# Planner durations of the attention heads, keys of image 1's attention and input projections, and delta's projections paired in two row halves of TensorE

## The chip, the cores and the metric

The kernel runs on one core of a Trainium2 chip. Its metric is device time in microseconds (us), the median of several runs. A core has these engines: TensorE (PE, matrix products and transposes through a 128 x 128 array, results in PSUM), VectorE (DVE), ScalarE (ACT), GpSimd (POOL), and SyncE (SP), which here issues every transfer between memory and the core. Each engine works through its own list of instructions in order and waits at an instruction until the semaphores it needs are there.

## The reference, cut to what matters

Two images of 48 x 48 tokens with 768 channels. Layer 0 is neighbourhood attention, layer 1 a selective scan in both directions. Everything is float32.

```python
def attention(x):                      # 12 heads of 64, keys: the 7 x 7 neighbourhood
    q, k, v = split(x @ w_qkv)
    attn = softmax(q * 64 ** -0.5 . k[neighbours])
    return (attn . v[neighbours]) @ w_out

def scan_branch(x, z):                 # forward; once more on the reversed tokens
    x = silu(depthwise_conv4(x))       # 1536 channels, 2304 tokens
    dt, B, C = split(x_proj_w @ x)     # 48, 16, 16 rows
    delta = softplus(dt_proj_w @ dt + dt_proj_b)
    h[t] = exp(delta[t] * A) * h[t-1] + delta[t] * x[t] * B[t]   # 16 states per channel
    return (sum_n(h * C) + x * Dp) * silu(z)

x = x + attention(group_norm(x))
x = x + out_proj(scan_branch(in_proj(group_norm(x))) + reversed_scan_branch(...))
```

## The kernel before

**Tiling.** The scan works in units. A unit is one tile of 128 channels (`k`, 12 tiles) in one chunk of 384 tokens (`i`, 6 chunks), in one direction (`back`), of one image (`b`): 2 x 2 x 6 x 12 = 288 units, in this order. Image 0 forward is units 0 to 71, image 0 backward 72 to 143, image 1 forward 144 to 215, image 1 backward 216 to 287. A unit has four groups of four states. For each group (`scan`, `group`) the buffer `hb` is filled with delta * x * B (line 1254, on DVE or on POOL), ACT makes exp(delta * A) for each state into the PSUM buffers `da` (line 1276), DVE scans two states at a time (line 1287), POOL multiplies by C (line 1302), and PE adds the states up by transposing them into the bank `py` (line 1319). ACT takes `py` out to `yt` (line 1345). In the backward direction PE turns the sum of both directions back (line 1372), and DVE multiplies by silu(z) (line 1382).

**Delta.** For every three tiles (`KB`) `deltas_of` fetches `u` and the 49 rows (48 and a bias) of the weights `dtw`, multiplies them on PE with the rows `dt` of the chunk (line 1180), one product of 49 x 128 by 49 x 384 for each tile, and ACT copies each result out (line 1186). Softplus over the three (line 1191) needs another table of ACT functions, so there are two table loads about it. The results of line 1180 use the PSUM pool `mm`, which has two banks. The same two banks serve all projections, and, in image 1's attention, its scores, transposes and weighted values too (`BESIDE`).

**Attention.** `project` makes q, k and v of a tile of 384 tokens, `core` and `block` fetch what a block of 8 x 16 queries needs, and `heads` computes two columns of queries of two heads: scores on PE (line 784, two heads in the two row and column halves of the array), a masked maximum on DVE (line 794), exponentials with their sum on ACT (line 800), the reciprocal on DVE (line 815), the scaling on ACT or DVE (lines 843, 849), transposes on PE (line 825), their copy (line 831), the weighted values on PE (line 879), and their copy (line 893). Image 0's attention comes before the scan and has the scan's buffers (`FIRST`). Image 1's attention runs beside image 0's scan. After it come image 1's input projections with the convolution (`in_proj`: PE line 387, ACT line 957, DVE line 964, ACT line 990) and their projections to dt, B and C (`x_proj`).

**What sets the order.** Each operation is recorded with `add(engine, ns, fn, key, reads, writes, ...)`: an assumed duration, a key in units (when it is due), and what it reads and writes. `Order.run` then plans all engines together. It takes the operation that can start first by the assumed durations, ranks by start and key, looks 2.5 units ahead of the oldest unfinished unit, and allots buffers. In the program the instructions of each engine stand in the planned order; on the chip they start when their waits allow it. A fill of groups 1 to 3 may go to DVE or POOL, as the plan finds one free first (`alt`). Where PE would be idle for more than 800 ns in the plan, filler transposes are put there (line 1520). Assumed durations come from `mm`, `act` and `dve`, plus a constant written at the place.

The keys around the change, with lines of the file before:

```python
    A0, A1, P1 = (-56, -16), (50, 118), 118          # attention of image 0, of image 1, input projections
    ...
            attention(b, *A1, True, BESIDE)
    ...
            start = P1 + 12 * i if b else 9 * (i - 1) - 4
            end = start + (ND - 2 if b else 8)
```

Of the kernel before, what the change touches and what calls it, by code (L numbers as in the profile page):

```python
# [16 lines left out]
P = 128  # L17
# [13 lines left out]
NKEY = WR * WC  # L31
# [3 lines left out]
UU = 2  # L35
# [6 lines left out]
RK = 48  # L42
XD = RK + 2 * NS
CL = 384
CHUNKS = [(l, CL) for l in range(0, L, CL)]
# [205 lines left out]
def tile_kernel(  # L251
# [282 lines left out]
    def attention(b, start, end, job, T):  # L534
# [234 lines left out]
        def heads(n, p, i, u, kcs, ks, qs, vs, vat, mask, to, key):  # L769
# [20 lines left out]
            for v in range(UU):  # L790

                def masked(v=v):

                    nc.vector.tensor_tensor_reduce(  # L794
                        pr[:, v, :], scv(v), mask[:, v * NKEY : (v + 1) * NKEY], -1.0, 3.0e38,
                        ALU.add, ALU.min, sm[:, v : v + 1],
                    )
# [7 lines left out]
                add("DVE", dve(NKEY) + 160, masked, key, r=[sc, mask], w=[(pr, v), (sm, v)], **S)  # L805
                add(
                    "ACT", act(NKEY, 1) + 230, exponentials, key, r=[(pr, v), (sm, v)],
                    w=[(pr, v), (sm, UU + v)], **S,
                )
# [44 lines left out]
            if job:  # L854
                add("PE", UU * NK * 110 + 60, lambda: turned(range(UU)), key, r=[pr], w=[pt, pT], **S)
                add(
                    "ACT", act(UU * NK * P) + 30, lambda: taken(range(UU), nc.scalar.copy), key, r=[pt],
                    w=[pT], **S,
# [14 lines left out]
            def weighted():  # L873
# [11 lines left out]
            marks["pv"] = add(  # L885
                "PE", 900, weighted, key, r=[*((x[0], x[1]) for x in vs), pT], w=[po, to], **S
            )
# [11 lines left out]

            add("ACT" if job else "DVE", act(P) + 60, kept, key, r=[po], w=[to], **S)  # L900

# [7 lines left out]
    def in_proj(b, i, start, end, conv=True, gate=True, nk=KB, tags=("uz",), banks=("mm",), proj=None):  # L909
# [78 lines left out]
        def finish(k0, nk, uz, dsts, key):  # L988
# [3 lines left out]

            add("ACT", 2600 + act(len(dsts) * nk * cl), silu, key, r=[uz], w=[uz], job=True)
            for s, dst in enumerate(dsts):
# [162 lines left out]
    def deltas_of(ch, k0, x):  # L1157
# [17 lines left out]
        )  # L1175
        for j in range(KB):
            acc = ps("mm", f"dl_{n}_{j}")
            add(
                "PE", mm(1, cl),
                lambda j=j, acc=acc: nc.tensor.matmul(  # L1180
                    acc[:, c], w[:, j * P : (j + 1) * P], dt[:, c], start=True, stop=True
                ),
                at + 0.01 * j, r=[dt, w, u], w=[acc, (dl, j)], early=EARLY,
            )
            add(
                "ACT", act(cl), lambda j=j, acc=acc: nc.scalar.copy(dl[:, j, c], acc[:, c]),  # L1186
                at + 0.01 * j, [acc], [(dl, j)], early=EARLY,
            )

# [202 lines left out]
    def chunk(b, back, i, at):  # L1392

        l0, cl = CHUNKS[i]
        s = f"{b}_{back}_{i}"
        dt = sb("dt", [RK + 1, CL], s)
        src = xd[back][b]
        add(
            "SP", 400, lambda: nc.sync.dma_start(dt[:, :cl], src[: RK + 1, l0 : l0 + cl]), at - 1.4,
            [(src, cols(l0, cl))], [dt], size=RK * cl * 4,  # L1400
        )
        bc = []
# [54 lines left out]
    for b in range(nb):  # L1457
# [113 lines left out]
```

## Time and profile before

| | |
|---|---|
| Time, median of 3 runs | 7049.78 us (7040.85 to 7054.37) |
| Profiled execution | 7040.0 us |
| Its span, from first to last instruction | 7038.2 us |
| Mean granted clock of TensorE | 0.976 |
| Instructions | 108877 |
| Scans on DVE (line 1287) | 2304, mean 1749 ns |
| Fills (line 1254) | 650 on DVE, mean 1746 ns; 502 on POOL, mean 3203 ns |
| Multiplies on POOL (line 1302) | 1152, mean 3186 ns |
| Delta's projections (line 1180) | 576 records (two for each product) |
| Filler transposes (line 1520) | 5124 |

A row of the profile's groups names line, engine, operation, what is written from what, the shapes and the count, then the busy time and the mean of one, then the idle time of the engine just before and what ended it. The mean of one includes a tail that overlaps with the next instruction of the same engine; from start to start two scans are 1.66 us apart. PE means products, PEld the loading of their stationary operand. Idle time costs only where it is on the path that sets the end.

### The profile page before, as it was taken

The numbers are of one execution on the slowest core, as the hardware profiler recorded it, in microseconds if no ns is written. First come the engines' busy times: TensorE is split into PE (matmuls) and PEld (weight loads), VectorE is DVE, ScalarE is ACT, GpSimd is POOL, SyncE is SP. The second block draws the span as 40 slices with busy tenths as digits, with TensorE's granted clock in tenths as the row PEclk, the third lists the DMA queues.
The fourth block names the chain that finished last, engine by engine and source line by source line (L and its number), as shares of the span: only waits on it lengthen the run. The fifth ranks groups of instructions, "written<-read, shape, count | busy, mean of one in ns | idle before, by whom it ended". The sixth has DMA issues, their size and how long they took to land. (4 is left out here: it accounts for less than half of the span.)

```text
span 7038.2 us, 108877 instructions
## 1 busy us (share of the span) xinstructions
PE 6280.1 (89%) x40140; PEld 4878.2 (69%) x40140; DVE 5990.5 (85%) x6102; ACT 4851.3 (69%) x10516; POOL 5468.5 (78%) x1958
## 2 busy tenths in 40 slices
PE   8999899899899989899988888888888898999888
PEld 5666656666667767666766666666678887777777
DVE  1343459999999989878899999999999999999998
ACT  1222248878887777677877777788876667777774
POOL 0000019898889989777889999999999999999997
PEclk9999999999999999999999999999999999999999
DMA  6666454544565455555542443343466676655553
GB/s 194 185 214 190 143 174 131 153 137 133 162 190 162 148 165 166 161 175 155 179 152 87 137 138 89 95 143 114 139 179 191 175 218 198 192 176 160 163 171 104
DMA packets 1348293, 1115.48 MB, mean 158 GB/s; under 512 B 137840, under 2 KB 1338000, under 8 KB 1347728
## 3 DMA queue, kind: packets, MB, share of 16 engines
q1 hardware_dynamic: 1347760, 1108.50, 52.6%
q8 instruction: 318, 5.21, 0.3%
q14 instruction: 215, 1.76, 0.1%
HBM read 895.34 MB, written 213.57 MB: 158 GB/s over the span
## 5 line engine op out<-in xcount | busy, mean ns | idle before, releaser
L1287 DVE TENSOR_TENSOR_SCAN hb<-da,hb 128x772 f32<-128x772 f32 x2304 | 3923.6, 1749 | 200.1 <-ACT da L1276 148.8
L1302 POOL TENSOR_TENSOR hb<-hb,bc 128x1536 f32<-128x1536 f32 x1152 | 3652.7, 3186 | 379.4 <-DVE hb L1287 287.9
L1276 ACT ACTIVATE da<-dlt,A 128x384 f32<-128x384 f32 x4608 | 2677.4, 584 | 962.5 <-DVE hb L1287 884.9
L1319 PE MATMUL py<-ident,hb 128*128 128x128 f32 x13824 | 1750.0, 279 | 313.5 <-POOL hb L1302 306.6
L1319 PEld LDWEIGHTS py<-ident,hb 128*128 128x128 f32 x13824 | 1566.1, 143 | 570.5 <-POOL hb L1302 471.7
L1254 POOL TENSOR_TENSOR hb<-u,bc 128x1544 f32<-128x1544 f32 x502 | 1606.8, 3203 | 48.7 <-PE py L1319 42.6
L1254 DVE TENSOR_TENSOR hb<-du,bc 128x1544 f32<-128x1544 f32 x650 | 1131.3, 1746 | 37.3 <-ACT du L1231 27.5
L1204 POOL TENSOR_TENSOR u<-dlt,u 128x384 f32<-128x384 f32 x288 | 263.6, 917 | 478.0 <-ACT dlt L1191 386.9
L1520 PE MATMUL py<-ident 128*128 128x128 f32 x5124 | 630.8, 277 | 0.0
L387 PE MATMUL mm_xin<-xc,w_x 128*128 128x390 f32 x1656 | 592.6, 501 | 29.8 <-DVE uz_u L964 12.6
L387 PE MATMUL mm_z<-xc,w_z 128*128 128x384 f32 x1728 | 607.6, 492 | 6.3 <-ACT dlt L1186 3.8
L1520 PEld LDWEIGHTS py<-ident 128*128 128x128 f32 x5124 | 586.8, 143 | 17.3 <-issue 13.6
L387 PE MATMUL mm_out<-stage_y,w_o 128*128 128x192 f32 x3168 | 558.0, 330 | 18.9 <-DMA w_o<-in_w_opT 6.5
L387 PEld LDWEIGHTS mm_out<-stage_y,w_o 128*128 128x128 f32 x3168 | 519.0, 193 | 30.5 <-ACT dlt L1186 10.6
L930 POOL MEMSET xc<- 128x18 f32 x4 | 0.5, 118 | 630.0 <-PE mm_v L387 630.0
L964 DVE SCALAR_TENSOR_TENSOR uz_u<-mm_xin,conv_w,uz_u 128x384 f32<-128x384 f32 x792 | 427.9, 610 | 45.6 <-ACT uz_u L957 44.0
L387 PEld LDWEIGHTS mm_xin<-xc,w_x 128*128 128x128 f32 x1656 | 306.3, 193 | 230.2 <-issue 28.8
L387 PE MATMUL mm_qk<-xc_xn,w_qk 128*128 128x384 f32 x1296 | 452.8, 495 | 8.7 <-DVE sm L794 2.6
L387 PEld LDWEIGHTS mm_z<-xc,w_z 128*128 128x128 f32 x1728 | 314.8, 192 | 192.4 <-issue 9.4
L387 PEld LDWEIGHTS mm_qk<-xc_xn,w_qk 128*128 128x128 f32 x1296 | 238.6, 192 | 161.8 <-issue 15.9
L1260 ACT COPY bc<-state 128x8 f32<-128x8 f32 x960 | 183.0, 196 | 143.9 <-DVE hb L1254 68.3
L800 ACT ACTIVATE pr<-pr,sm 128x196 f32<-128x196 f32 x432 | 194.0, 450 | 126.4 <-DVE sm L794 124.8
(163 smaller groups left out, 6454.8 us busy)
## 6 DMA issues: line engine op xcount, KB each, us to landing
w_o<-in_w_opT SPq DMA_DIRECT2D x264, 384.0 KB
bc<-xdf SPq DMA_DIRECT2D x96, 768.0 KB
bc<-xdb SPq DMA_DIRECT2D x96, 768.0 KB
w_qk<-in_w_qkv SPq DMA_DIRECT2D x144, 384.0 KB
w_x<-in_w_inT SPq DMA_DIRECT2D x144, 384.0 KB
w_z<-in_w_inT SPq DMA_DIRECT2D x144, 384.0 KB
w_ao<-in_w_out SPq DMA_DIRECT2D x72, 384.0 KB
u<-uf SPq DMA_DIRECT2D x48, 576.0 KB
```

What stands on the lines that cost most here:

```text
L387: nc.tensor.matmul(acc[:m, o0 : o0 + cl], wb[:, wi, wo : wo + m], xb[:, xi, xo : xo + cl], start=c == 0, stop=c == n - 1,)
L800: nc.scalar.activation(pr[:, v, :], pr[:, v, :], AF.Exp, bias=sm[:, v : v + 1], scale=-1.0, accum_out=sm[:, UU + v : UU + v + 1],)
L930: nc.gpsimd.memset(xc[:, :, : a - lo], 0.0)
L964: nc.vector.scalar_tensor_tensor(u, px[:, at[j] : at[j] + cl], q["conv_w"][:, k, j : j + 1], u, ALU.mult, ALU.add,)
L1204: lambda j=j: nc.gpsimd.tensor_mul(u[:, j, h], dl[:, j, c], u[:, j, h]), at + 0.06 + 0.25 * j,
L1254: on.tensor_mul(cells(hb, SG), by.unsqueeze(1).to_broadcast([P, SG, W]), bc[g].ap)
L1260: "ACT", 98, lambda: nc.scalar.copy(bc[g][:, :, ends], was), now - 0.4,
L1276: lambda: nc.scalar.activation(cells(da, 2)[:, j % 2, h], dl[:, jd, c], AF.Exp, scale=q["A"][:, k, i : i + 1]),
L1287: lambda: nc.vector.tensor_tensor_scan(flip(hb[at2]), flip(da[:, : 2 * W]), flip(hb[at2]), 0.0, ALU.mult, ALU.add),
L1302: lambda: nc.gpsimd.tensor_mul(cells(hb, SG)[:, :, h], cells(hb, SG)[:, :, h], bc[NSG + g][:, :, c]),
L1319: nc.tensor.matmul(py[:tp, t * P : (t + 1) * P], cells(hb, SG)[:, j, h][:, tb[t]], ident, start=False, stop=g == NSG - 1 and j == SG - 1 a ...
L1520: nc.tensor.matmul(marks["py"][:, CL : CL + P], ident, ident, start=False, stop=False, is_transpose=True, skip_group_check=True,)
```

## The change

The change has three parts. None alters what is computed.

1. The assumed durations in `heads` are other constants, and so are those of the silu in `in_proj` and of the product u * delta on POOL. They alter the plan, not the instructions themselves.
2. Image 1's attention is keyed from unit 46 to 124 (78 units) where it was 50 to 118 (68), and image 1's input projections begin at 124 with 11 units between chunks where they began at 118 with 12.
3. The weights `dtw` and the rows `dt` are fetched twice, to partitions 0 to 48 and to partitions 64 to 112. Of a group of three tiles the first two are multiplied in one operation of the plan, tile 0 from the lower half of the rows and tile 1 from the upper half, into two banks of `mm`; the third is alone, in the lower half. Before, each of the three was an operation of its own.

```diff
+ROW = 64
...
-                add("DVE", dve(NKEY) + 160, masked, key, ...)
+                add("DVE", dve(NKEY) + 22, masked, key, ...)
-                    "ACT", act(NKEY, 1) + 230, exponentials, key, ...
+                    "ACT", act(NKEY, 1) + 130, exponentials, key, ...
-                        "DVE", 198,
+                        "DVE", 70 if job else 150,
-                        "ACT", act(NKEY, 1) + 40,
+                        "ACT", act(NKEY, 1) + 35,
-                    "ACT", act(UU * NK * P) + 30, lambda: taken(range(UU), nc.scalar.copy), ...
+                    "ACT", act(UU * NK * P), lambda: taken(range(UU), nc.scalar.copy), ...
-                "PE", 900, weighted, key, ...
+                "PE", 640 if job else 750, weighted, key, ...
-            add("ACT" if job else "DVE", act(P) + 60, kept, key, ...)
+            add("ACT" if job else "DVE", act(P) if job else 230, kept, key, ...)
...
-            add("ACT", 2600 + act(len(dsts) * nk * cl), silu, key, ...)
+            add("ACT", 2750 + act(len(dsts) * nk * cl), silu, key, ...)
...
-        u, w = sb("u", [P, KB, CL + 2], n, KB), sb("dtw", [RK + 1, KB * P], n)
+        u, w = sb("u", [P, KB, CL + 2], n, KB), sb("dtw", [ROW + RK + 1, KB * P], n)
...
-            nc.sync.dma_start(w.ap, q["dtT"][:, k0 * P : (k0 + KB) * P])
+            for r in (0, ROW):
+                nc.sync.dma_start(w[r : r + RK + 1], q["dtT"][:, k0 * P : (k0 + KB) * P])
...
-        for j in range(KB):
-            acc = ps("mm", f"dl_{n}_{j}")
-            add(
-                "PE", mm(1, cl),
-                lambda j=j, acc=acc: nc.tensor.matmul(
-                    acc[:, c], w[:, j * P : (j + 1) * P], dt[:, c], start=True, stop=True
-                ),
-                at + 0.01 * j, r=[dt, w, u], w=[acc, (dl, j)], early=EARLY,
-            )
-            add("ACT", act(cl), lambda j=j, acc=acc: nc.scalar.copy(dl[:, j, c], acc[:, c]), ...)
+        for j0 in range(0, KB, 2):
+            js = range(j0, min(j0 + 2, KB))
+            accs = [ps("mm", f"dl_{n}_{j}") for j in js]
+
+            def raw(js=js, accs=accs):
+                for j, acc in zip(js, accs):
+                    r = slice(j % 2 * ROW, j % 2 * ROW + RK + 1)
+                    nc.tensor.matmul(
+                        acc[:, c], w[r, j * P : (j + 1) * P], dt[r, c], start=True, stop=True
+                    )
+
+            add(
+                "PE", mm(1, cl) * (1.6 if len(js) > 1 else 1.2), raw, at + 0.01 * j0, r=[dt, w, u],
+                w=[*accs, *((dl, j) for j in js)], early=EARLY,
+            )
+            for j, acc in zip(js, accs):
+                add("ACT", act(cl), lambda j=j, acc=acc: nc.scalar.copy(dl[:, j, c], acc[:, c]), ...)
...
-                "POOL", 960,
+                "POOL", 850,
                 lambda j=j: nc.gpsimd.tensor_mul(u[:, j, h], dl[:, j, c], u[:, j, h]), ...
...
-        dt = sb("dt", [RK + 1, CL], s)
+        dt = sb("dt", [ROW + RK + 1, CL], s)
-        add("SP", 400, lambda: nc.sync.dma_start(dt[:, :cl], src[: RK + 1, l0 : l0 + cl]), at - 1.4, ...)
+        def rows():
+            for r in (0, ROW):
+                nc.sync.dma_start(dt[r : r + RK + 1, :cl], src[: RK + 1, l0 : l0 + cl])
+
+        add("SP", 800, rows, at - 1.4, ...)
...
-    A0, A1, P1 = (-56, -16), (50, 118), 118
+    A0, A1, P1 = (-56, -16), (46, 124), 124
...
-            start = P1 + 12 * i if b else 9 * (i - 1) - 4
+            start = P1 + 11 * i if b else 9 * (i - 1) - 4
```

More of the change, by code (lines that the diff above doesn't have):

```diff
@@ L803, in exponentials @@
                     )
-                add("DVE", dve(NKEY) + 160, masked, key, r=[sc, mask], w=[(pr, v), (sm, v)], **S)
+                add("DVE", dve(NKEY) + 22, masked, key, r=[sc, mask], w=[(pr, v), (sm, v)], **S)
                 add(
-                    "ACT", act(NKEY, 1) + 230, exponentials, key, r=[(pr, v), (sm, v)],
+                    "ACT", act(NKEY, 1) + 130, exponentials, key, r=[(pr, v), (sm, v)],
                     w=[(pr, v), (sm, UU + v)], **S,
@@ L856, in heads @@
                 add(
-                    "ACT", act(UU * NK * P) + 30, lambda: taken(range(UU), nc.scalar.copy), key, r=[pt],
+                    "ACT", act(UU * NK * P), lambda: taken(range(UU), nc.scalar.copy), key, r=[pt],
                     w=[pT], **S,
@@ L885, in heads @@
             marks["pv"] = add(
-                "PE", 900, weighted, key, r=[*((x[0], x[1]) for x in vs), pT], w=[po, to], **S
+                "PE", 640 if job else 750, weighted, key, r=[*((x[0], x[1]) for x in vs), pT], w=[po, to], **S
             )
@@ L898, in kept @@
                 )
-            add("ACT" if job else "DVE", act(P) + 60, kept, key, r=[po], w=[to], **S)
+            add("ACT" if job else "DVE", act(P) if job else 230, kept, key, r=[po], w=[to], **S)
         project(0)
@@ L991, in silu @@
                 nc.scalar.preload_act_table_set("natural_log_exp_and_others")
-            add("ACT", 2600 + act(len(dsts) * nk * cl), silu, key, r=[uz], w=[uz], job=True)
+            add("ACT", 2750 + act(len(dsts) * nk * cl), silu, key, r=[uz], w=[uz], job=True)
             for s, dst in enumerate(dsts):
@@ L1175, in deltas_of @@
         )
-        for j in range(KB):
-            acc = ps("mm", f"dl_{n}_{j}")
-            add(
-                "PE", mm(1, cl),
-                lambda j=j, acc=acc: nc.tensor.matmul(
-                    acc[:, c], w[:, j * P : (j + 1) * P], dt[:, c], start=True, stop=True
-                ),
-                at + 0.01 * j, r=[dt, w, u], w=[acc, (dl, j)], early=EARLY,
-            )
-            add(
-                "ACT", act(cl), lambda j=j, acc=acc: nc.scalar.copy(dl[:, j, c], acc[:, c]),
-                at + 0.01 * j, [acc], [(dl, j)], early=EARLY,
-            )
+        for j0 in range(0, KB, 2):
[7 more added lines that the diff above has]
+                    )
+            add(
+                "PE", mm(1, cl) * (1.6 if len(js) > 1 else 1.2), raw, at + 0.01 * j0, r=[dt, w, u],
+                w=[*accs, *((dl, j) for j in js)], early=EARLY,
+            )
+            for j, acc in zip(js, accs):
+                add(
+                    "ACT", act(cl), lambda j=j, acc=acc: nc.scalar.copy(dl[:, j, c], acc[:, c]),
+                    at + 0.01 * j, [acc], [(dl, j)], early=EARLY,
+                )
         def softplus():
@@ L1395, in chunk @@
         s = f"{b}_{back}_{i}"
-        dt = sb("dt", [RK + 1, CL], s)
+        dt = sb("dt", [ROW + RK + 1, CL], s)
         src = xd[back][b]
[L1398 to L1401, printed above, removed]
+        def rows():
+            for r in (0, ROW):
+                nc.sync.dma_start(dt[r : r + RK + 1, :cl], src[: RK + 1, l0 : l0 + cl])
+        add("SP", 800, rows, at - 1.4, [(src, cols(l0, cl))], [dt], size=2 * RK * cl * 4)
         bc = []
```

## The prediction

> **What bounds the kernel now.** I read the page's parts 1 and 2 first. The first fence has the busy sums, then PE's and DVE's busy tenths in 40 slices of 176 us.
>
> ```profile
> PE 6280.1 (89%) x40140; PEld 4878.2 (69%) x40140; DVE 5990.5 (85%) x6102; ACT 4851.3 (69%) x10516; POOL 5468.5 (78%) x1958
> PE   8999899899899989899988888888888898999888
> DVE  1343459999999989878899999999999999999998
> ```
>
> PE's busy time includes 5124 filler transposes (line 1520), so it is no measure of need. DVE is lightly used in the first six slices (image 0's attention, PE's own stretch), is at 9 almost everywhere afterwards, and dips in slices 14 to 19. I mapped time to units of scan work (a unit is one tile of 128 channels in one chunk, 288 in all) by putting the scans of the trace beside the scans in DVE's instruction order: unit 84 starts at 2814.0 us, unit 108 at 3405.4. A unit takes 18.9 us in the last stages and 24.6 us between those two points. The next view is the stretch view for units 84 to 107, and for comparison units 144 to 155 (columns: length, then busy time of PE, PE loads, DVE, ACT, POOL, then clock and DMA).
>
> ```profile
> core 0: us, PE busy (x) PEld busy (x) DVE busy (x) ACT busy (x) POOL busy (x), PEclk, DMA share, GB/s
> 2814.00:3405.00 591.00, 542.03 (x3815) 405.29 (x3813) 480.73 (x543) 431.93 (x1102) 457.04 (x163) 0.97 0.53 163
> 4201.40:4450.30 248.90, 211.76 (x1435) 170.65 (x1434) 242.53 (x200) 190.95 (x359) 235.56 (x85) 0.99 0.35 107
> ```
>
> In the second stretch DVE (97%) and POOL (95%) bound. In the first DVE is at 81%, POOL at 77%, and PE at 92% with no filler at all: image 1's attention and the scan share PE there, and PE sets the pace. The waits of that first stretch say the same; columns are the sum, how often, the longest.
>
> ```profile
> POOL hb L1254 <- PE py L1319: 42.6, 11, 8.3
> ACT yt L1345 <- PE py L1319: 23.0, 5, 9.9
> DVE pr L794 <- PE mm_s L784: 17.7, 7, 9.0
> DVE xr_x L712 <- PE mm_ao L387: 15.2, 8, 3.3
> ```
>
> POOL waits for hb buffers that PE's add-up transposes free too late, and DVE waits for scores and output products. Last, the timeline, for what the edited operations cost.
>
> ```profile
> 3001.24 0.36 DVE L794 CUSTOM_DVE_ANT_0 pr<-mm_s,mask 128x196 f32<-128x196 f32 x1
> 3001.52 0.36 DVE L794 CUSTOM_DVE_ANT_0 pr<-mm_s,mask 128x196 f32<-128x196 f32 x1
> 3011.76 0.88 PE L784 MATMUL mm_s<-uz_k,xpw_q 64*64 64x196 f32 x8
> 4339.56 1.55 PE L1180 MATMUL mm_dl<-dt,dtw 49*128 49x384 f32 x4
> ```
>
> A masked maximum takes 0.28 us from start to start, which is what the new estimate says (55 + 204 + 22 ns); the old one said 0.42. Eight score records in quarter tiles take 0.81 us to the next instruction, where one after the other they would take twice that: in the records, two of different halves start 0.007 us apart, two of the same half 0.16. Two delta projections (four records, 0.323 us each) take 1.48.
>
> **What the Trainium skill says.** TensorEngine Tiling (Array Packing), Key Properties: tiles work independently, but a change of tiling mode drains TensorE. The trace agrees on both: 0.007 us as above, and going from a 128-row transpose to a 49-row delta and back adds some 0.09 + 0.10 + 0.09 = 0.29 us (0.202 for 0.109 before it, 0.427 for 0.323 in it, 0.413 after). Same page, Gotcha 1: different row tiles write different PSUM banks, so a pair needs both banks of the pool mm. ScalarE: Activation LUTs, What ACT_TABLE_LOAD costs: back-to-back activations overlap by about 93 ns; here L800 has a mean of 450 ns and 349 from start to start, so the new estimates, which look 90 ns short of the page, are the true spacing. Perfetto Trace Analysis, Optimization Strategy: regimes with different bounds gain by interleaving; that is what the attention's keys decide, and the stretches above are such regimes.
>
> **The change, part by part.** No arithmetic is added. In the two instruction orders DVE keeps its work but for three fills that go to POOL (650 to 647, 502 to 505); ACT has the same instructions; PE loses 177 fillers; SP gains 120 issues. So what counts is where the work lies.
>
> *Keys and estimates* (one answer). The attention of image 1 still starts at unit 51 and ends at unit 123, not 118; input projections go from units 120-186 to 124-188, and their first result is ready at unit 135, needed at 144. Units 84 to 107 on PE, counted in both orders, by the spacing of the records: value products 324 to 216 at 0.224 us, -24.2; query and key products 180 to 186 at 0.646, +3.9; scores 168 to 164 at 0.203, -0.8; attention transposes 168 to 160 at 0.109, -0.9; weighted values 336 to 304 at 0.077, -2.5; deltas (below) -2.2. Sum -26.7. At 92% busy that is -29 us of time. DVE's work there falls by 10 to 461 us, 82% of the 562 that are left, so PE still sets the pace and nothing is late next.
>
> *Elsewhere DVE decides*, so I take its change of work, from the same count (scan and fill 1.665 us each, conv tap 0.525, masked 0.281): units 60-71 +6; 72-83 -1, and PE is relieved by 21 of 228, for which I take 3 of DVE's 23 us idle, together -4; 108-119 -9; 120-131 +2 and the attention's waits that come along, +4; 132-143 +5; 144-191 +11 (951 to 962: input projections that came later); units 0-59 and 192-287 -8. The attention's own waits on DVE (17.7 + 15.2 + 9.0 on L815, 42 us in units 84-107) should fall with its density: 67 to 72 units, 7% less in that stretch and the ones beside it, and estimates that are right; I take -6, bounds 0 and -42.
>
> *Delta pairs.* A lone pair has records at 0, 0.32, 0.33, 0.65 and ends near 0.97 instead of 1.29: -0.32 x 96 groups; mode entries rise from 163 to 181, +5 in all. So -26 us of PE in the whole kernel, most of it under filler and worth nothing; -2.2 counted above. The pair must find both mm banks empty. Behind it on PE stand the add-up transposes, and POOL's fills wait for those. Price of one wait: from 0 to ACT's copy (0.47) behind a softplus with its two table loads (1.28 + 1.17 + 1.28), 4.2 us. Eight groups lie in units 84-107: 0 to +34 us; I take 0.5 each, +4, as the order puts 1.3 us or more of other work between the last use of a bank and half of the groups. Elsewhere PE has 11 to 70 us of filler per 12 units, which covers it; without that cover it would cost 40 more.
>
> *DMA.* The second copies of dtw (73.5 KB, 96) and dt (24) add 9 MB to 1115, and 120 issues of 0.39 us, 47 us, to an SP queue that issues for 2141 us, 30% of the span. Each later issue on SP moves by 0.4 us. PE waited for dtw for 5.6 us in all; fetches are keyed 0.7 units, 14 us, ahead. Taken as nothing, at most 37 us if every group waited its 0.39.
>
> *Image 0's attention* has the same PE work (838 to 837 us) and about the same distance between its steps on PE (median from scores to transposes 3.3 before, 3.7 after): 0, bounds -15 and +15.
>
> Sum: -29 - 4 - 9 + 6 + 4 + 5 + 11 - 8 - 6 + 4 = -26 us. The profiled run took 7040.0 us (span 7038.2, 1.8 around it), so it would be 7014; the median of the runs shown is 9.8 higher, and on that base I forecast 7024.
>
> **Rivals.** *Nothing gained* (about 7045): DVE's total work is unchanged, and what leaves units 84-107 makes DVE busier in 120-191, where it idles only 2 to 5%. For it: the +26 us of that list. Against it: DVE idles 110 us of 591 in the PE-bound stretch, and that is what shrinks. *More than that* (about 6970): with right estimates the whole of units 72-119, where DVE idles 14% by its busy time, comes to the 5 to 9% of units 0 to 71: -80. For it: the longest waits for PE are single ones of 8 to 10 us, a matter of PE's order more than of its amount of work. Against: PE remains almost without filler there. *Slower* (about 7080): the old estimates left slack. They were 0.40 us long on DVE, 0.3 on ACT and 0.27 on PE per head, 108 heads. Now scores and masked maxima stand closer, DVE is in order, and each masked maximum that comes before its scores holds the scans, and behind them POOL's multiplies. The price of one such wait in the trace is 17.7 / 7 = 2.5 us; from 11 more of them the gain is gone, and at one for every fourth head and the 0 to 34 us of the pairs it is +30 to +60. Against it: distances from scores to transposes grow on PE (median 6.1 to 7.0 us in image 1). *The pairs do not overlap*: then PE's -26 us becomes +5, some 3 us in the PE-bound stretch, not visible.
>
> **How the numbers follow.** What I forecast has a chance of 0.52, its own range 7000 to 7038; nothing gained 0.13; more 0.18; slower 0.17. This kernel's runs spread by 0.2%, which I take as the bound of no change, 7036 to 7064. Faster: 0.49 of the first and 0.18, 0.67; same: 0.03 + 0.13 + 0.02, 0.18; slower 0.15. The range leaves out 0.06 below 6965 (half of "more" is above it) and 0.14 above 7062.
>
> **What would show it.** The stretch between the first scans of units 84 and 108: I expect about 563 us for 591, PE still over 90% and almost no filler. If PE has fallen to 85% with the length unchanged, my PE bound is wrong. Units 120-191 should take 12 to 20 us more. In the delta rows, records of one pair should start 0.007 us apart once; if it is 0.32 they do not overlap. Waits of PE for ACT's dlt copy (43.5 us in all ahead of the deltas) should grow by less than 50 us; DVE's wait for scores (L794) should not grow. The first scan should still start near 1021 us. Wrong would be: DVE waiting for scores by 50 us more, or PE for the two banks by microseconds a group.

## The result and the profile after

The changed kernel takes 7037.08 us (median of 16 runs, 7022.65 to 7050.09); the kernel before took 7050.06 us beside it (16 runs). The ratio is 0.9983, with a 95% interval of [0.9976, 0.9990]. So it is 13 us (0.17%) faster, about half of the 26 us of the forecast's sum; the interval leaves out 1, but the gain is smaller than the 0.2% that the prediction set as its bound of no change.

The profiled execution took 7037.3 us, its span is 7035.5 us. The profiled execution of before lay 10 us below its kernel's median, that of after lies on its median, so the two spans differ by 2.7 us only. The busy sums and the tenths of the kernel after:

```profile
PE 6233.1 (89%) x39963; PEld 4848.2 (69%) x39963; DVE 5972.3 (85%) x6099; ACT 4852.0 (69%) x10516; POOL 5477.4 (78%) x1961
PE   8999889888989899999988788888988898989888
DVE  1343349989999989888889999999999999999997
```

Nothing that must be done has changed much: PE lost fillers, and DVE's sum is within 0.3% of that of before. DVE's tenths have no 7 left in the middle, where before there was one in the dip, and its sixth slice is at 4 for 5: the scan starts later. Where the time went is read by laying the scans of each trace beside the order of scans in DVE's list, as in the prediction. Lengths in us between the first scans of units:

| units | before | after | difference | forecast |
|---|---|---|---|---|
| start to first scan | 1020.8 | 1047.4 | +26.7 | 0 |
| 0-59 | 1293.4 | 1303.6 | +10.2 | with 192-287: -8 |
| 60-71 | 243.7 | 248.0 | +4.3 | +6 |
| 72-83 | 256.1 | 250.3 | -5.8 | -4 |
| 84-107 | 591.4 | 528.7 | -62.7 | -29 |
| 108-119 | 284.2 | 277.8 | -6.4 | -9 |
| 120-143 | 511.7 | 518.8 | +7.1 | +9 |
| 144-191 | 987.5 | 1008.3 | +20.8 | +11 |
| 192-287 | 1849.3 | 1852.6 | +3.3 | see 0-59 |

The forecast's other two terms, waits of the attention (-6) and of the deltas (+4), had no stretch of their own. Two rows are far from their forecast: units 84 to 107 gained twice as much, and 27 us were lost before the first scan, where nothing was expected. After the first scan the profile's time fell from 6017.5 to 5988.1 us, by 29 us, close to the whole forecast.

The stretch view for units 84 to 107 and 144 to 155 after (length, then busy time of each engine; last clock and DMA):

```profile
core 0: us, PE busy (x) PEld busy (x) DVE busy (x) ACT busy (x) POOL busy (x), PEclk, DMA share, GB/s
2849.38:3378.05 528.67, 487.65 (x3455) 366.34 (x3456) 465.78 (x505) 414.83 (x1047) 465.10 (x165) 0.97 0.54 167
4174.60:4427.20 252.60, 210.40 (x1413) 171.79 (x1414) 240.94 (x199) 194.83 (x364) 238.35 (x86) 0.97 0.36 110
```

In the first line PE is busy for 92% (487.65 of 528.67), as before (542.03 of 591.00): the length followed PE's work, which fell by 54 us and not by 27. DVE rose from 81% to 88%. The waits of that stretch after (sum, how often, longest):

```profile
DVE pr L795 <- PE mm_s L785: 14.4, 6, 6.5
...
POOL hb L1263 <- PE py L1328: 12.5, 3, 6.5
...
ACT yt L1354 <- PE py L1328: 3.2, 5, 1.3
```

POOL's wait for `hb` buffers behind PE's add-up fell from 42.6 to 12.5 us, ACT's for `py` from 23.0 to 3.2, DVE's for scores from 17.7 to 14.4.

The loss is ahead of the first scan. There image 0's attention is PE's own stretch. The waits of PE in the first 1000 us of the kernel before:

```profile
PE da L825 <- DVE pT L831: 20.1, 21, 1.0
PE py_po L879 <- DMA bc_v<-vd: 11.5, 25, 1.7
PE da L784 <- DVE sm L794: 3.1, 6, 1.0
```

and of the kernel after (`da` is here the bank of scores and transposes, `py_po` that of the weighted values):

```profile
PE da L826 <- DVE pT L832: 30.5, 28, 2.3
PE py_po L880 <- DMA bc_v<-vd: 17.8, 27, 5.3
PE da L785 <- DVE sm L795: 15.1, 21, 0.8
PE da L785 <- DMA bc_q<-qd: 5.3, 1, 5.3
PE da L826 <- DVE pr L850: 4.9, 14, 1.0
```

PE waits longer for DVE's copy `pT` and for its masked maxima, in more waits than before, of 1.1 and 0.7 us on the mean. Summing the gaps between PE's records up to image 0's last output product gives 55.6 us before and 84.8 after, +29, as much as the loss; PE's busy time up to there is the same (828 and 826 us). Last, the timeline of PE for a delta pair, its single third tile, and the add-up transposes between them:

```profile
3010.29 0.92 PE L1185 MATMUL mm_dl<-dt,dtw 49*128 49x384 f32 x4
3011.13 1.53 PE L1328 MATMUL py<-ident,hb 128*128 128x128 f32 x12
3013.37 0.91 PE L1185 MATMUL mm_dl<-dt,dtw 49*128 49x384 f32 x2 [0.71 <-ACT dlt L1195]
3014.21 0.69 PE L880 MATMUL mm_po<-pT,uz_kv 98*64 98x64 f32 x16
```

From the pair's start to the next instruction are 0.84 us, as for the single product (3013.37 to 3014.21). In the timeline before, two products took 1.48.

### The profile page after: what moved, and what is told of

Read it like the earlier page. It is cut to its first block, busy times and chain, and to the rows that moved or that the text cites. A ratio compares the mean times of both kernels' runs of the same rounds, so it can differ in the third digit from the quotient of the medians.

```text
span 7035.5 us, 108705 instructions
## 1 busy us (share of the span) xinstructions
PE 6233.1 (89%) x39963; PEld 4848.2 (69%) x39963; DVE 5972.3 (85%) x6099; ACT 4852.0 (69%) x10516; POOL 5477.4 (78%) x1961
## 4 chain that ended last, share of the span: by engine, by line
DVE 38%; PE 20%; ACT 15%; POOL 13%; issue 10%; DMA 5%; SPq 1%; DVEq 0%; POOLq 0%; ACTq 0%
DVE hb L1296 25%; POOL hb L1311 8%; DVE hb L1263 7%; ACT da L1285 4%; PE mm_qk L388 4%; POOL hb L1263 4%; DVE uz_u L965 3%; PE py L1328 2%; PE mm_ao L388 2%; PE mm_v L388 2%; PE mm_xin L388 2%; PE da L785 1%; DMA bc<-xdb 1%; PE mm_out L388 1%; PE mm_z L388 1%
## 5 line engine op out<-in xcount | busy, mean ns | idle before, releaser
L1531 PE MATMUL py<-ident 128*128 128x128 f32 x4947 | 615.5, 279 | 0.0
L1531 PEld LDWEIGHTS py<-ident 128*128 128x128 f32 x4947 | 570.8, 144 | 27.0 <-issue 22.7
L388 PEld LDWEIGHTS mm_out<-stage_y,w_o 128*128 128x128 f32 x3168 | 516.7, 192 | 38.4 <-DVE xr L1109 13.4
L1344 PE MATMUL py<-ident,vt 128*128 128x128 f32 x864 | 154.6, 289 | 147.3 <-ACT yt L1354 146.7
```

Of the source, the lines that this page charges most:

```text
L388: nc.tensor.matmul(acc[:m, o0 : o0 + cl], wb[:, wi, wo : wo + m], xb[:, xi, xo : xo + cl], start=c == 0, stop=c == n - 1,)
L1344: nc.tensor.matmul(py[:tp, t * P : (t + 1) * P], vt[:, tb[t]], ident, start=t == 0, stop=False, is_transpose=True, skip_group_check=True,)
L1531: nc.tensor.matmul(marks["py"][:, CL : CL + P], ident, ident, start=False, stop=False, is_transpose=True, skip_group_check=True,)
```

## The experiments

Each starts from the kernel after, except where the text says so. Ratios are to the kernel before, run beside it; that of after is 0.9983.

### Image 0's assumed durations old

Theory 1: with durations that fit, PE's in-order list in image 0's attention lost its slack, and this cost the 27 us ahead of the first scan. Rival: it is scatter of that stretch, or comes from the other parts of the change.

```diff
-                add("DVE", dve(NKEY) + 22, masked, ...)
+                add("DVE", dve(NKEY) + (22 if job else 160), masked, ...)
-                    "ACT", act(NKEY, 1) + 130, exponentials, ...
+                    "ACT", act(NKEY, 1) + (130 if job else 230), exponentials, ...
-                        "DVE", 70 if job else 150,
+                        "DVE", 70 if job else 198,
-                "PE", 640 if job else 750, weighted, ...
+                "PE", 640 if job else 900, weighted, ...
-            add("ACT" if job else "DVE", act(P) if job else 230, kept, ...)
+            add("ACT" if job else "DVE", act(P) if job else act(P) + 60, kept, ...)
```

> The changed kernel, but image 0's attention is planned with the old durations (masked maximum +160, exponentials +230, reciprocal 198, weighted values 900); all else as changed. Theory 1, lost slack: the shorter durations put image 0's steps so close that TensorE waits in order for DVE's copies and maxima; the first scan comes back from 1047 to about 1021 us, TensorE's idle time ahead of it from 124 to about 95 us, and the whole takes about 25 us less than the changed kernel, 7010 to 7015 on the base of 7050. Rival, chance of one execution (the granted clock, transfers): the first scan stays within 5 us of 1047 or the median within 8 us of 7037.

Measured: 7014.12 us (5 runs), ratio 0.9954 [0.9941, 0.9966]. The first scan starts at 1025.5 us. PE's waits in the first 1000 us of this kernel:

```profile
PE da L826 <- DVE pT L832: 20.1, 21, 1.0
PE py_po L880 <- DMA bc_v<-vd: 14.6, 23, 2.1
PE da L785 <- DVE sm L795: 4.1, 6, 1.2
```

The waits for `pT` are those of before to the digit, those for the maxima nearly, and PE's gaps sum to 57.0 us. Only constants of the plan were edited, so the order they produce is the cause. Nor is it scatter: up to the last weighted values of image 0, PE's order in this kernel is that of before and of the four kernels with wider keys below, and the order of the kernel after is also that of the four in which image 1's durations, the keys or the pairs are undone. In the six profiles of the first order PE's gaps sum to 52 to 57 us, in the five of the second to 79 to 85. Against the kernel after it is 0.9983 - 0.9954 = 0.29%, some 20 us: without its new durations for image 0 the change gains 32 us.

### Which of the durations: the chain on DVE and ACT, or the weighted values on PE

The first of two kernels keeps PE's 750 ns for the weighted values and takes back the other four edits of the diff above; the second takes back PE's alone:

```diff
-                "PE", 640 if job else 750, weighted, ...
+                "PE", 640 if job else 900, weighted, ...
```

> The changed kernel, with image 0's durations on VectorE and ScalarE old (masked maximum, exponentials, reciprocal, copy of the result) and only TensorE's weighted values new (750). Theory 1, slack of the chain: TensorE waits because scores and transposes are planned just when the vector engines are done; then these durations hold most of the gain of e1, the first scan is near 1025 to 1032 us and the median within 8 us of 7014. Theory 2, TensorE's own duration: nothing comes back, the first scan stays at 1047 to 1060 us, the median near 7037.

> The counterpart: only the weighted values of image 0 are planned with the old 900, the vector engines' durations as changed. Theory 1, slack of the chain: the first scan stays at 1045 to 1060 us and the median near 7037. Theory 2, TensorE's own duration: near 1025 us and 7014.

Measured: with DVE's and ACT's durations old 7016.19 us (5 runs), ratio 0.9955 [0.9940, 0.9970], first scan at 1026.0 us, PE's waits for `pT` 17.2 us and for the maxima 4.2. With PE's alone old 7054.04 us (20 runs), ratio 1.0011 [1.0004, 1.0017], first scan at 1069.5 us, the same waits 29.8 and 13.4. PE's gaps sum to 58.7 us in the first and 91.1 in the second, so it is the durations of the chain of maximum, exponentials, reciprocal and copy: two orders made with the old ones and two with the new ones agree on it. That the longer durations make the plan put other work on PE between a step of a head and the next was not counted. The second kernel is also 20 us slower than the kernel after, which neither theory expected: with the new chain, one more constant of the plan moves the time by as much again.

The new durations are not wrong: a masked maximum is 0.28 us from the next in the trace, and from its start to that of its exponentials are 0.40 to 0.41 us in half of the 216 cases (the rest wait longer), where the plan has 0.416. A plan with exact durations puts the next PE instruction where its input is just ready, and each small lateness then stops PE. That small latenesses are the reason is argued; that the durations of this chain are is shown.

### More slack than before

If slack is what counts, more of it may help more. Image 0's durations go as far above the old ones as these are above the new:

```diff
-                add("DVE", dve(NKEY) + 22, masked, ...)
+                add("DVE", dve(NKEY) + (22 if job else 298), masked, ...)
-                    "ACT", act(NKEY, 1) + 130, exponentials, ...
+                    "ACT", act(NKEY, 1) + (130 if job else 330), exponentials, ...
-                        "DVE", 70 if job else 150,
+                        "DVE", 70 if job else 250,
-                "PE", 640 if job else 750, weighted, ...
+                "PE", 640 if job else 1050, weighted, ...
-            add("ACT" if job else "DVE", act(P) if job else 230, kept, ...)
+            add("ACT" if job else "DVE", act(P) if job else act(P) + 120, kept, ...)
```

> The kernel of e1 with about twice the added slack in image 0's durations (masked maximum +298, exponentials +330, reciprocal 250, weighted values 1050). If TensorE's waits for VectorE in image 0's attention come from too little distance in the plan, they fall again: lines 785 and 826 waited 23 us before the change and 46 after it, and here 20 us or less; the first scan comes at 1015 to 1028 us, the median at 7005 to 7018. If the old constants were only a lucky order, the first scan falls anywhere, over 1035 us as likely as not.

Measured: 7029.10 us (16 runs), ratio 0.9976 [0.9969, 0.9984], first scan at 1041.6 us. The expectation failed. PE's waits in the first 1000 us:

```profile
PE py_po L880 <- DMA bc_v<-vd: 20.7, 40, 1.4
PE da L826 <- DVE pT L832: 10.7, 11, 1.0
PE da L826 <- DVE sm L816: 9.8, 6, 3.3
```

The wait for `pT` halved, as slack should make it, but waits for the values' transfers (14.6 to 20.7) and for the reciprocal (3.2 to 9.8) grew in its place, and PE's gaps are 65.0 us. Of the 16 us by which the first scan comes later than with the old durations, 8 are these gaps; the rest is that PE's own records took longer (841 for 833 us), as they also do between profiles of one order (see the last section). The expectation had put a first scan behind 1035 us on the side of a lucky order, so this run doesn't decide between slack and luck: the wait that slack should shorten got shorter, the whole did not. The old durations are better than the new ones and than these; no rule for the amount of slack is shown.

### Image 1's durations old

```diff
-                add("DVE", dve(NKEY) + 22, masked, ...)
+                add("DVE", dve(NKEY) + (160 if job else 22), masked, ...)
-                    "ACT", act(NKEY, 1) + 130, exponentials, ...
+                    "ACT", act(NKEY, 1) + (230 if job else 130), exponentials, ...
-                        "DVE", 70 if job else 150,
+                        "DVE", 198 if job else 150,
-                "PE", 640 if job else 750, weighted, ...
+                "PE", 900 if job else 750, weighted, ...
...
-            add("ACT", 2750 + act(len(dsts) * nk * cl), silu, ...)
+            add("ACT", 2600 + act(len(dsts) * nk * cl), silu, ...)
-                "POOL", 850,
+                "POOL", 960,
```

The scaling, the copies of `pT` and `to` on ACT have their old constants too.

> The changed kernel, but image 1's attention, the silu and the product u * delta planned with the old durations; image 0's durations, keys and pairs as changed. Theory 1, the keys: units 84 to 107 owe their 63 us to the 78 units over which the attention is keyed, so they stay near 530 to 545 us, and the whole near 7037 to 7050. Theory 2, the estimates: the 34 us beyond the load that left come from durations that are right, and the stretch takes 560 us or more here, the whole 7065 or more.

Measured: 7049.94 us (13 runs), ratio 1.0007 [0.9999, 1.0015], 0.24% or 17 us above the kernel after. Units 84 to 107 take 532.0 us (528.7 with the new durations): they don't make that stretch. The new plan is worth something elsewhere, 12 us after the first scan in the profiles (6000 to 5988): units 60-83 16 longer, but 108-143 13 and 192-287 15 shorter. So the new durations of image 1 pay, and those of image 0 do not. That PE has other work there to put between the steps of a head is the likely reason, and is argued.

### The keys old

```diff
-    A0, A1, P1 = (-56, -16), (46, 124), 124
+    A0, A1, P1 = (-56, -16), (50, 118), 118
-            start = P1 + 11 * i if b else 9 * (i - 1) - 4
+            start = P1 + 12 * i if b else 9 * (i - 1) - 4
```

> The changed kernel with the old keys (attention of image 1 from 50 to 118, input projections from 118 by 12 units). Theory 1, the keys: units 84 to 107 go back to 575 us or more, units 120 to 191 get 15 to 20 us shorter, the whole takes 7060 to 7080. Theory 2, the estimates: the stretch stays below 560 us and the whole within 15 us of 7037.

Measured: 7045.60 us (13 runs), ratio 1.0001 [0.9993, 1.0010]. The stretch view for units 84 to 107 (columns as above):

```profile
2853.43:3425.27 571.84, 526.99 (x3790) 399.06 (x3788) 481.70 (x535) 425.61 (x1086) 460.60 (x165) 0.98 0.56 170
```

571.8 us against 528.7 with the new keys, again at 92% of PE: 43 of the 63 us of that stretch are the keys. But units 108-143 take 783.7 (after: 796.5) and 144-191 take 987.7, as before the change (after: 1008.3). The new keys lose 33 of their 43 us there, in units in which DVE is the bound and into which they move work. By the medians the keys are worth 0.18%, 13 us (5 to 20 by the two intervals); by the two profiles the time after the first scan is 2 us shorter (5988.1 for 5990.0), so where these 13 us lie isn't shown.

### Delta's projections one by one, and the pair without overlap

The first kernel fetches `dt` and `dtw` once and makes each product an operation of its own, as before the change. The second keeps the pair as one operation, its two fetches and the order of every engine; its two products only read the same half of the rows:

```diff
-                    r = slice(j % 2 * ROW, j % 2 * ROW + RK + 1)
+                    r = slice(0, RK + 1)
```

> The changed kernel with delta's three products as three single operations of the lower rows, one fetch of dtw and dt each. Theory 1: the pairs are worth nothing, since TensorE has filler nearly everywhere and only some 2 us of them lie in units 84 to 107: within 8 us of 7037, units 84 to 107 within 8 us of 529. Theory 2, both banks: each pair makes TensorE wait, and without them it is 10 to 30 us faster, most of it in units 0 to 59 and 144 to 191. Theory 3, the pairs relieve TensorE where it is the bound: 15 us slower or more, in units 84 to 107.

> The changed kernel with the same order of instructions on every engine, but both products of a pair read the lower rows, so that TensorE cannot run them side by side. The records of a pair then start 0.32 us apart and the pair takes 1.48 us instead of 1.0, 96 times: 46 us more work on TensorE. Theory 1, the overlap itself is nearly worthless, since filler or idle time covers it outside units 84 to 107: the median lies within 6 us of 7037, and what e2 lost came with its other plan. Theory 2, the overlap pays for itself: 12 us slower or more.

Measured: one by one 7047.56 us (13 runs), ratio 1.0006 [0.9998, 1.0014], 0.23% or 16 us above the kernel after. That is the size of the third theory but not its place: units 84 to 107 take 536.8 us, 8 longer. And that kernel has another plan, so it doesn't price the pair alone. Without overlap, in the same order: 7042.11 us (21 runs), ratio 0.9991 [0.9985, 0.9998], some 5 us above the kernel after; the two intervals overlap, so the overlap is worth between nothing and some 12 us. The same pair in its timeline:

```profile
3019.01 1.55 PE L1185 MATMUL mm_dl<-dt,dtw 49*128 49x384 f32 x4
3020.50 1.53 PE L1328 MATMUL py<-ident,hb 128*128 128x128 f32 x12
```

1.49 us to the next instruction, for 0.84 with the two halves. With 96 pairs the overlap saves PE up to 96 x 0.64 = 61 us (an upper bound: many pairs are cut up by waits), and few of them reach the end; in units 84 to 107 the length is the same (528.8 and 528.7). The rest of the 16 us came with the other edits of the first kernel: the plan that one operation for two tiles gives, and the second fetches.

### Wider keys

If 43 us came from spreading the attention over more units, more width should give more, until image 1's input projections come too late: they are keyed behind it, and its first scan is unit 144. Four kernels take image 0's old durations (the first experiment) and wider keys; here the first:

```diff
-    A0, A1, P1 = (-56, -16), (46, 124), 124
+    A0, A1, P1 = (-56, -16), (46, 130), 130
-            start = P1 + 11 * i if b else 9 * (i - 1) - 4
+            start = P1 + 10 * i if b else 9 * (i - 1) - 4
```

> The kernel of e1 with image 1's attention keyed over 84 units (46 to 130) and the input projections from 130 by 10 units. Theory 1, TensorE's load sets units 84 to 107: the stretch gets shorter once more, 505 to 520 us for 527, until VectorE's own 460 us of work and its usual 7 per cent set it; units 108 to 191 get 10 to 20 us longer, the whole 7000 to 7020. Theory 2, the stretch is already at VectorE's bound: it stays within 5 us of 527 and the whole takes 7020 to 7035.

The others have 132, 128 and 136 in place of both 130.

> The kernel of e8 with image 1's attention from 46 to 132 and the input projections from 132 by 10 units. TensorE's load in units 84 to 107 falls a little further: 495 to 507 us for 506.7. Theory 1, late projections: the first chunk of image 1 gets its dt, B and C just at unit 144, and units 132 to 155 take 15 us longer or more: 7005 to 7030 in all. Theory 2, no limit yet: 6993 to 7005.

> The kernel of e8 with 128 in place of 130, a neighbour that asks how much of its gain belongs to the one plan. If the gain follows the keys it lies between e1 and e8: 7000 to 7012, units 84 to 107 at 507 to 520 us. If e8 is one lucky order, it scatters to 7012 or more.

> Image 0's durations old as in the first experiment, image 1's attention keyed from 46 to 136, its input projections from 136 in steps of 10: four units later than the version with 132, which took 6983 us. Theory 1 (width is still worth more than lateness): stretch 84-107 at 465 to 482 us and a time of 6960 to 6978. Theory 2 (the turning point is passed: the projections of image 1's chunk 0 are due at 136 to 144 and needed at 144, so the scan waits for them): stretch 84-107 no shorter than 478, units 132 to 155 together 15 us or more longer than with 132, and a time of 6984 or more. Two plans that differ in nothing but these keys have scattered by some 8 us, so 6979 to 6983 decides nothing.

Measured, with the first experiment (124, steps of 11) as the base:

| end of keys | time, us | ratio to before | units 84-107 | 108-143 | 144-191 | 192-287 |
|---|---|---|---|---|---|---|
| 124 | 7014.12 | 0.9954 [0.9941, 0.9966] | 526.8 | 797.8 | 1007.8 | 1855.7 |
| 128 | 6993.32 | 0.9921 [0.9907, 0.9934] | 502.1 | 790.9 | 1016.5 | 1848.9 |
| 130 | 7001.38 | 0.9938 [0.9922, 0.9954] | 506.7 | 792.3 | 1023.2 | 1871.0 |
| 132 | 6983.41 | 0.9905 [0.9890, 0.9920] | 484.8 | 792.3 | 1019.9 | 1874.8 |
| 136 | 7261.14 | 1.0308 [1.0289, 1.0328] | 482.6 | 814.9 | 1136.0 | 1997.0 |

The version with 132 is the best of all, 64 us below the kernel before and 0.78% below the kernel after. In units 84 to 107 130 did what was expected of it; 132 went further than that (484.8 us), and 128 came out faster than its expectation and faster than 130, so neighbouring keys may also differ by what order the plan falls into, by some 10 us (the intervals of 128 and 130 overlap, with 4 runs each); the trend from 124 to 132 is larger. The stretch view with 132, for units 84 to 107:

```profile
2813.43:3298.20 484.77, 438.49 (x3256) 334.11 (x3254) 461.50 (x480) 402.34 (x1013) 450.12 (x161) 0.99 0.54 167
```

PE's work has fallen to 438 us, 90% of the length, and DVE's 461 are 95%: DVE is as near to the bound here as in the units behind it. With 136 both sums are the same (437 and 460 us), and so is the stretch; the wider key took no more work out of it, so the run doesn't tell which of the two bounds it. But with 136 the projections are too late. The waits of units 144 to 203 with 136 (4117 to 5620 us):

```profile
POOL u L1213 <- ACT dlt L1200: 259.1, 6, 124.3
DVE hb L1263 <- ACT du L1240: 128.7, 10, 59.3
ACT ev L1065 <- PE mm_xd L388: 120.9, 11, 45.9
```

POOL waits for delta's softplus and DVE for the row products that follow it, once for 124 us; behind them stands ACT's copy of the projections to dt, B and C (`mm_xd`), which came out when its chunk's scan was due: for each of the five chunks from unit 144 to 192 the last of these copies ends 15 to 39 us ahead of the chunk's first scan. With 132 it ends 24 us ahead for the first chunk, and 69 to 167 for the third to fifth. Four units of key cost 278 us. The expectation had the sign, and only the smaller part of the size and place: units 132 to 155 took 77 us more than with 132, but units 180 to 203 took 207 more, with the longest wait.

## Why the prediction was right or wrong

**The forecast as a whole.** Its sum was -26 us; the medians give -13, inside the likeliest case's own range of 7000 to 7038, by one microsecond. That is in part luck: errors of both signs cancelled, 34 us more were gained in one stretch, and 27, 21 and 10 lost in others. (In the chances, half of *more* is 0.09, where the text on the range has 0.06.)

**Keys and estimates: the principle right, the size off.** PE did set the pace of units 84 to 107 and still does at 92%, as the prediction had it, and DVE's 466 us are near its 461. The term that was mis-sized is PE's work there, forecast -26.7 us and measured -54. By tiles, from the sum of PE's records in the two stretches: value products -20.3 (forecast -24.2), query and key products -14.0 (forecast +3.9), output products -8.5 (none forecast), scores -7.3 (-0.8), weighted values -3.5 (-2.5), deltas -2.9 (-2.2), transposes -1.9 (-0.9); fillers and the rest +4. The count was taken between the first add-up transposes of units 84 and 108 in PE's list, the time between their first scans on DVE. Between those transposes the trace has PE's work at 536.7 us before and 506.9 after, -30, and the length at 578.6 and 545.8, -33, close to the forecast. The other 30 us are how far PE lags behind DVE at the two ends: from the first scan to the first add-up transpose 34 us before and 12 after at unit 84, 21 and 29 at unit 108. Between the two scans, 54 / 0.92 = 59 of the 63 us follow from PE's work. That the keys bring it was right (43 of 63 us), though the prediction did not part them from the estimates.

**Elsewhere DVE decides: right for units 60-83 and 108-143, short for the rest.** There each row is within 3 us of its forecast. Units 120 to 191 together took 28 us more, where the signs had 12 to 20. Units 144-191 took +20.8 for +11: DVE's busy time rose from 957.4 to 968.3 us, which is the +11 of the count, and the other 10 are waits that no count of work shows. They are DVE's waits for ACT's exponentials in this stretch, before and after:

```profile
DVE hb L1287 <- ACT da L1276: 14.5, 13, 2.1
```

```profile
DVE hb L1296 <- ACT da L1285: 27.9, 18, 5.9
```

The -8 for units 0-59 and 192-287 was wrong by 21 us (+13.5): in units 0-59 DVE's work fell by 3 us, but its idle time grew from 83.9 to 97.2. No single wait carries it (DVE's for `da` went from 49.5 to 52.9, for `du` from 6.4 to 8.7), and these units took 1299 to 1309 us in every variant of the kernel after, whichever part was undone. What of it is the plan stays open.

**Delta pairs: the pair is twice as good, and worth as little as said.** The prediction let the products overlap once, -0.32 us for each lone pair. In the trace both passes overlap: of the 96 pairs, 45 have their four records at 0, 0.007, 0.427 and 0.434 (within 2 ns), and the next instruction then mostly at 0.846, while the others are pulled apart by waits; without overlap they stand at 0, 0.427, 0.749 and 1.072 with the next at 1.485: -0.64. In the Trainium skill, TensorE: Matmul & The Clock Gate, Part 3: Packing small matmuls, Measured speedup vs the span model, a pack has the length of one product and about 4 ns for each further tile; the trace agrees (0.846 for 0.84). PE's wait for the `dlt` copy ahead of the deltas grew from 43.5 to 65.8 us, inside the 50 that were allowed. That little of PE's saving would reach the end was right: some 5 us are left of it, if any.

**DMA.** PE's waits for `dtw` grew from 5.6 to 15.0 us, within the 37 that bounded them; there is no sign of SP as a bound.

**Image 0's attention: the step that failed.** It was put at 0 with bounds of 15 us either way, because PE had the same work and the median distance from scores to transposes grew (3.3 to 3.7). The profile shows +26.7, and the experiment with image 0's durations puts some 20 to 22 us of it to that edit. A median of distances in an order doesn't tell how many of its steps have none to spare; there are more waits of under a microsecond (21 for 6 on line 785), and nothing but PE sets the length of this stretch.

**The rivals.** By the number alone *nothing gained* (about 7045) is nearer than the forecast's 7024, and its mechanism was at work: 33 of the 43 us of the keys came back in later units. It falls only in that the later units did not take all. *More* falls too, though wider keys with the old head reach its mechanism, DVE's idle time of the zone gone (110 us before, 63 after, 23 with 132). *Slower* named the mechanism that fits what was measured, durations without slack that stop an engine in order, but the wrong place: it was looked for on DVE in image 1's attention, where the wait for scores fell, and it sits on PE in image 0's. *The pairs do not overlap* is refuted by the records.

## What to carry to other kernels

Durations in a planner that writes an order for in-order engines also decide how much slack that order has. Here, where one engine alone sets the pace, durations that are exact to 10 ns cost time, and old ones that were some 0.1 us too long were better; still longer ones were not. So test the constants of each stretch on their own, as exactness alone doesn't make the better order. Spread a burst of work on the engine that bounds one stretch until the engine that bounds its neighbours is near its bound there too, and watch when its last product is due, as passing that point cost four times the largest gain. Count the work of a stretch between the same two events by which its time is taken.

## What the runs showed of the hardware

Two products of 49 rows in the two row halves of PE take the time of one, 0.846 us for 0.84, in float32 with two records for each product; 1.485 one after the other. This was not expected to be complete.

In the tail of image 0's attention, where PE waits more often, its granted clock is lower. The stretch view of the kernel after (columns as above, the clock behind POOL's sum):

```profile
0.00:750.00 750.00, 674.03 (x4033) 460.07 (x4034) 245.39 (x946) 160.59 (x489) 1.60 (x11) 0.98 0.62 189
750.00:938.40 188.40, 151.62 (x1249) 105.01 (x1247) 79.59 (x348) 47.32 (x168) 0.00 (x0) 0.91 0.46 137
```

The granted clock is 0.98 in the first 750 us and 0.91 in the rest, where PE is busy 80% of the time. In the Trainium skill, TensorE: Matmul & The Clock Gate, Part 1: The HAM clock gate, HAM oscillation, the rule is that PE should have no idle gaps of more than some 3.4 us, since such a gap sets its clock to half. The trace differs in the length of the gap. The same tail of the kernel before, and PE's longest waits in its first 1000 us; the first of them is the start of the kernel:

```profile
750.00:911.30 161.30, 137.66 (x1163) 91.78 (x1161) 80.19 (x340) 45.18 (x161) 0.00 (x0) 0.92 0.52 156
PE mm_gna L453 <- DVE gn_mva L448: 28.3, 1, 28.3
PE da L825 <- DVE sm L815: 4.9, 5, 2.3
```

After its start PE never waits longer than 2.3 us there, and the clock of the tail is 0.92 all the same. Which pattern of short gaps does it is not shown: between kernels the clock doesn't follow PE's busy share (0.86 at 85% with image 0's old durations, 0.91 at 80% in the kernel after). The tail's clock was 0.83 to 0.92 from one profile to the next, also between kernels with the same order in this stretch. In the five profiles of the order of the kernel after, PE's records up to the last output product take 826 to 842 us and the first scan lies between 1047 and 1060; in the six profiles of the order of before they take 828 to 840, and it lies between 1021 and 1030. So a single profile tells the time of that stretch to some 10 us only, while the sums of PE's gaps keep the two orders apart.
